# Layer 0's selective scan: VectorE weighs each scan's states one scan later, with five state buffers

## The chip, the cores and the metric

The kernel runs on one core of a Trainium2 chip. The metric is the device time of one execution in microseconds (us); the kernel before takes 15601.95 us, the median of three runs (15600.6 to 15609.41). Five engines work side by side, each through its own instructions in order: TensorE (PE, with its weight loads PEld), VectorE (DVE), ScalarE (ACT), GpSimd (POOL) and SyncE (SP), which issues DMAs. They wait for one another through semaphores.

## The reference

The program is four layers over an image of 2 x 64 x 64 positions with 128 channels; only layer 0 is touched. Its core is a selective scan along four orders of the 4096 positions of each image (kk = 0 to 3; orders 2 and 3 run backward, 1 and 3 by columns), with 256 channels and 16 states for each:

```
def step(h, inp):
    ut, dt, bt, ct = inp
    dA = jnp.exp(dt[..., None] * A4)
    h = dA * h + (dt * ut)[..., None] * bt[:, :, None, :]
    y = jnp.einsum('bkdn,bkn->bkd', h, ct)
    return (h, y)
```

The results of the four orders, each with u * D added, are summed into one Y.

## The kernel before, in words

For each of the two images `layer0` first computes U (channels on partitions, two halves of 128), then runs the scan stage (lines 247 to 420), then normalises Y and projects it. The stage walks 32 chunks of T = 512 positions, in the order kk = 0, 2, 1, 3 and eight chunks each (`todo`, line 330); a chunk walks its 16 states n. One state's tiles hold both halves, 128 x 2 x 512 numbers. One state is:

- POOL: S = du * (row n of B) (line 376), then for all but a direction's first chunk the state carried over from the chunk before is added into one column (lines 381, 382). `du` is dt * u; rows of B come by DMA, four at a time, in `br`.
- ACT: dA = exp(dt * A) in two halves (line 385), into one of two PSUM tiles `dAs`.
- DVE: the scan over both halves, in place in S (line 387).
- ACT: a copy of the last column of the state before into `stt`, for the next chunk (line 389).
- DVE: M = S * (row n of C) (line 401). The row, `pcn`, is a PSUM tile that TensorE fills by a product of `cs` with a selector (`c_row`, line 343). There is one such tile, so the next row waits for M to have read it.
- PE: the row of the next state, then four passes that add both halves of M into the PSUM tile `yp` through the identity (line 419).

At n = 0 `add_up` (line 346) first adds the finished `yp` of the chunk before into Y: for kk 0 by two ACT copies (line 354), for kk 2 by two DVE additions (line 356), for kk 1 and 3 by two strided ones (line 350). There is one `yp` tile, so only then can two products with `dd` (line 398) start the new one with u * D.

Beside the states runs the `prologue` of a later chunk (line 260), a generator; a step of it is issued after each state's M. It starts at n = 12 for the chunk two ahead: two steps copy U into `uc` (ACT), one makes the product `px`, one copies it to `xd` and `cs` and sends B's rows to DRAM, and in the next chunk's states follow softplus for dt (ACT with two table loads, and POOL at lines 299, 308, 311, 318, 320) and du (POOL, line 322).

The order on every engine is the order of the program text (`manual_schedule`, line 358). S has four buffers, M three.

Of the kernel before, what the change touches and what calls it, by code (L numbers as in the profile page):

```python
# [16 lines left out]
F32 = mybir.dt.float32  # L17
# [3 lines left out]
ALU = mybir.AluOpType  # L21
# [4 lines left out]
P = 128  # L26
# [132 lines left out]
def layer0(k):  # L159
    tc, nc, ins, X = k.tc, k.nc, k.ins, k.X  # L160
    T = N
    NC = L // T
    with ExitStack() as es:
# [34 lines left out]
        for b in range(B):  # L198
            Xb = X[:, b * NTB : (b + 1) * NTB, :]
            with ExitStack() as e2:  # L200
                pre = e2.enter_context(tc.tile_pool(name=f"l0p{b}", bufs=1))
                wk = e2.enter_context(tc.tile_pool(name=f"l0w{b}", bufs=3))
# [44 lines left out]
            with ExitStack() as e2:  # L247
                ch = e2.enter_context(tc.tile_pool(name=f"l0h{b}", bufs=2))
                sm = e2.enter_context(tc.tile_pool(name=f"l0s{b}", bufs=1))
                wk = e2.enter_context(tc.tile_pool(name=f"l0k{b}", bufs=3))  # L250
# [9 lines left out]
                def prologue(kk, c, got):  # L260


                    uc = ch.tile([P, 2, T], F32, name="uc")
                    for h in range(2):
                        if kk % 2:
                            src = U[:, h, :].rearrange("p (g i w j) -> p w g j i", g=4, i=16, w=4)[:, c // 2, 2 * (c % 2) : 2 * (c % 2) + 2]
                            for g in range(2):
                                nc.scalar.copy(uc[:, h, g * 256 : (g + 1) * 256].rearrange("p (j i) -> p j i", j=16), src[:, g])
                        else:
                            src = U[:, h, (c // 2) * 1024 : (c // 2 + 1) * 1024].rearrange("p (i w j) -> p w i j", i=16, w=4)  # L270
                            for g in range(2):
                                nc.scalar.copy(uc[:, h, g * 256 : (g + 1) * 256].rearrange("p (i j) -> p i j", i=16), src[:, 2 * (c % 2) + g])
                        yield
                    px = ps.tile([P, N], F32, name="pd", tag="ps")
                    for h in range(2):
                        nc.tensor.matmul(px, w_xp[:, h, kk, :], uc[:, h, :], start=h == 0, stop=h == 1)
                    yield
                    xd = ch.tile([P, T], F32, name="xd")
                    nc.scalar.copy(xd, px)
                    bc = bcp.tile([16, T], F32, name="bc")  # L280
                    nc.sync.dma_start(out=bc, in_=xd[112:128, :])

                    cs = ch.tile([80, T], BF16, name="cs")
                    nc.scalar.copy(cs, xd[:80])


                    dt = ch.tile([P, 2, T], F32, name="dt")
                    du = ch.tile([P, 2, T], F32, name="du")
                    e = sm.tile([P, 2, T], F32, name="e")
                    u = sm.tile([P, 2, T], F32, name="u")  # L290
                    for h in range(2):
                        bias = k.v("dt_b")[:, kk * 2 + h : kk * 2 + h + 1]
                        pd = ps.tile([P, N], F32, name="pd", tag="ps")
                        nc.tensor.matmul(pd, w_dt[96:104, kk, h * P : (h + 1) * P], xd[96:104, :], start=True, stop=True)
                        yield
                        if h == 1:
                            yield
                            r = sm.tile([80, T], F32, name="r")
                            nc.gpsimd.tensor_tensor(r, xd[:80], cs, ALU.subtract)
                        nc.scalar.activation(e[:, h, :], pd, AF.Abs, bias=bias)  # L300
                        nc.scalar.activation(dt[:, h, :], pd, AF.Relu, bias=bias)
                    yield
                    nc.scalar.copy(cs[32:64], r[32:64])
                    nc.scalar.copy(cs[64:80], r[64:80])
                    nc.scalar.activation(e, e, AF.Exp, scale=-1.0)
                    yield
                    yield
                    nc.gpsimd.tensor_tensor(r[64:80], r[64:80], cs[64:80], ALU.subtract)
                    nc.scalar.activation(u, e, AF.Identity, bias=1.0)
                    yield  # L310
                    nc.gpsimd.tensor_tensor(dt, dt, e, ALU.add)
                    nc.scalar.copy(cs[64:80], r[64:80])
                    nc.scalar.activation(e, u, AF.Ln)
                    yield
                    nc.scalar.activation(u, u, AF.Identity, bias=-1.0)
                    yield
                    yield
                    nc.gpsimd.tensor_tensor(e, e, u, ALU.subtract)
                    yield
                    nc.gpsimd.tensor_tensor(dt, dt, e, ALU.add)  # L320
                    yield
                    nc.gpsimd.tensor_tensor(du, dt, uc, ALU.mult)

                    ea = ch.tile([P, 16, 2], F32, name="ea")
                    f = T - 1 if kk >= 2 else 0
                    for h in range(2):
                        nc.scalar.activation(ea[:, :, h], an[:, kk * 2 + h, :], AF.Exp, scale=dt[:, h, f : f + 1])
                    got.append((uc, bc, cs, dt, du, ea))

                todo = [(kk, ci) for kk in (0, 2, 1, 3) for ci in range(NC)]  # L330
                at = lambda i: (todo[i][0], NC - 1 - todo[i][1] if todo[i][0] >= 2 else todo[i][1])
                ready = []
# [8 lines left out]
                def c_row(cs, n):  # L341
                    o = pc_.tile([P, T], F32, name="pcn")
                    nc.tensor.matmul(o, sel[:, n, :], cs, start=True, stop=True)  # L343
                    return o

                def add_up(kk, c, yp):
                    for h in range(2):
# [3 lines left out]
                        else:  # L351
# [3 lines left out]
                            else:  # L355
                                nc.vector.tensor_tensor(o, yp[:, h, :], o, ALU.add)

                with tc.manual_schedule():
                    rows, pcn, last, save = spread(ready[0][1], 0), c_row(ready[0][2], 0), None, None
                    soon = []  # L360
                    for it, (kk, ci) in enumerate(todo):
                        c = at(it)[1]
                        uc, bc, cs, dt, du, ea = ready.pop()
# [8 lines left out]
                        for n in range(16):  # L372
                            if n % 4 == 0:
                                br = rows
                            S = wk.tile([P, 2, T], F32, name="S", bufs=4)
                            nc.gpsimd.tensor_tensor(S, du, br[:, n % 4, :].unsqueeze(1).to_broadcast([P, 2, T]), ALU.mult)  # L376
                            if ci > 0:
                                if n in (0, 2):

                                    m = slice(0, 14) if n == 0 else slice(14, 16)  # L380
                                    nc.gpsimd.tensor_tensor(stt[:, m], stt[:, m], ea[:, m], ALU.mult)
                                nc.gpsimd.tensor_tensor(S[:, :, f], S[:, :, f], stt[:, n, :], ALU.add)
                            dA = dAs[n % 2]
# [6 lines left out]
                                save = None  # L390
                            if ci < NC - 1:
                                save = stt[:, n, :], (S[:, :, 0] if kk >= 2 else S[:, :, T - 1])
                            if n == 0:
                                if last is not None:
                                    add_up(*last)
                                yp = py.tile([P, 2, T], F32, name="yp")
                                for h in range(2):
                                    nc.tensor.matmul(yp[:, h, :], dd[:, kk * 2 + h, :], uc[:, h, :], start=True, stop=False)
                                last = kk, c, yp
                            M = wk.tile([P, 2, T], F32, name="M")  # L400
                            nc.vector.tensor_tensor(M, S, pcn.unsqueeze(1).to_broadcast([P, 2, T]), ALU.mult)  # L401
                            if n == 12 and it + 2 < len(todo):
                                soon.append(prologue(*at(it + 2), ready))
                            for steps in soon:
                                next(steps, None)
                            if n == 14 and it + 1 < len(todo):
                                for _ in soon.pop(0):
                                    pass
                            if n < 15:
                                pcn = c_row(cs, n + 1)  # L410
                            elif ready:
                                pcn = c_row(ready[0][2], 0)
                            if n % 4 == 2:
                                if n < 14:
                                    rows = spread(bc, n // 4 + 1)
                                elif ready:
                                    rows = spread(ready[0][1], 0)
                            for h in range(2):
                                nc.tensor.matmul(yp[:, h, :], k.ident, M[:, h, :], start=False, stop=n == 15)  # L419
                    add_up(*last)  # L420

            with ExitStack() as e2:
                wk = e2.enter_context(tc.tile_pool(name=f"l0f{b}", bufs=3))
# [35 lines left out]
                behind = None  # L459
                for q in range(8):  # L460
# [3 lines left out]
                    behind = got  # L464
# [252 lines left out]
def layer2(k, x1, x3, rs, sh, wdr, mdr):  # L717
# [21 lines left out]
    with ExitStack() as es:  # L739
# [390 lines left out]
        def make_inputs(r):  # L1130
            i, r = divmod(r, 256 // R)
            if i < len(todo):
                d = r * R
                gi, q = divmod(d, DG)
                if q == 0:
                    Ss[i, gi] = sp.tile([P, 2, DG, T], F32, name="S")
                S = Ss[i, gi][:, :, q : q + R, :]
# [427 lines left out]
```

## Time and profile before

| | |
|---|---|
| three runs, median | 15601.95 us |
| the profiled execution's own time | 15611.47 us |
| its span, first to last instruction | 15609.7 us |
| granted TensorE clock, mean of the span | 0.913 |
| scan stage, first image | 143.0 to 2070.3 us |
| scan stage, second image | 2263.6 to 4194.7 us |
| POOL in both stages | 3279.03 us busy of 3858.40 |
| ACT in both stages | 2370.75 us busy |
| PE in both stages | 2577.80 us busy |

A group's line of the profile names the source line, the engine, the operation, the tiles written and read (`out<-in`), their shapes, how often it ran, then its busy time and the mean of one in ns, then the idle time of the engine just before these instructions, and what ended most of it. A line of a timeline has the start and the duration in us, and in brackets the idle time of the engine before it and what ended that. An engine's instructions may overlap a little in such rows, since a duration includes the end of the pipe.

### The profile page before, as it was taken

Reading aid. Unit: us, or ns where it says so; the run is one execution under the profiler, and the core shown is the slowest. Engines: PE = TensorE matmul, PEld = TensorE weight load, DVE = VectorE, ACT = ScalarE, POOL = GpSimd, SP = SyncE. Lnnn points to the kernel's source line nnn. Section 1 sums busy time; section 2 is a strip of 40 time slices with the busy share of each in tenths; the row PEclk is TensorE's granted clock in tenths of the full one; section 3 lists DMA queues with packets and bytes.
Section 4 is the critical chain, followed back from the end, with each engine's and each line's share of the span. In section 5 each row is a group of like instructions: output and inputs, shape, how many; then the busy total and the mean of one; then the engine's idle time right before and its main releaser. Section 6 shows DMA issues by size and latency. Waiting matters only on the chain.

```text
span 15609.7 us, 191436 instructions
## 1 busy us (share of the span) xinstructions
PE 11894.2 (76%) x69838; PEld 7117.6 (46%) x69838; DVE 13768.3 (88%) x12194; ACT 9829.7 (63%) x15891; POOL 13474.0 (86%) x5144
## 2 busy tenths in 40 slices
PE   6666676666677645486976978979788899898897
PEld 2222232222367512154653645646445555555565
DVE  7999979999853499999999999999999999999964
ACT  5666646666410177777777777777777777777752
POOL 6888848888578699999999999999999999999960
PEclk9999999999988767697987989989999999999998
DMA  2111111211175445465655556656666666666643
GB/s 82 71 71 70 67 60 71 73 68 71 63 226 160 137 151 163 154 195 177 204 188 169 195 179 194 202 182 200 194 193 195 192 197 202 192 196 199 188 160 130
DMA packets 1211438, 2373.47 MB, mean 152 GB/s; under 512 B 346744, under 2 KB 923896, under 8 KB 1044352
## 3 DMA queue, kind: packets, MB, share of 16 engines
q1 hardware_dynamic: 1163072, 2206.74, 43.2%
q0 software_dynamic: 46560, 153.18, 3.3%
q8 instruction: 552, 9.04, 0.2%
q14 instruction: 390, 3.19, 0.1%
q10 hardware_dynamic: 864, 1.32, 0.0%
HBM read 2018.49 MB, written 342.41 MB: 151 GB/s over the span
## 4 chain that ended last, share of the span: by engine, by line
POOL 35%; PE 14%; DVE 11%; DMA 3%; ACT 2%; issue 2%; SPq 0%; POOLq 0%; ACTq 0%; DVEq 0%
POOL S L1139 34%; DVE S L1195 10%; PE pef L1023 7%; PE Z L1157 2%; PE acc L996 2%; DMA row<-drow 2%; PE pw L822 1%; POOL S L1145 1%; ACT dA L1193 1%; ACT ze L1163 1%; DMA w<-in_w_b_dram 0%; PE acc L1058 0%; DMA e<-mdr 0%; ACT e L1003 0%; DMA w<-in_w_c_dram 0%
## 5 line engine op out<-in xcount | busy, mean ns | idle before, releaser
L1195 DVE TENSOR_TENSOR_SCAN S<-dA,S 128x512 f32<-128x512 f32 x8192 | 9226.4, 1200 | 397.2 <-ACT dA L1193 208.2
L1139 POOL TENSOR_TENSOR S<-row,g 128x4096 f32<-128x4096 f32 x1024 | 9102.2, 8895 | 280.6 <-DMA row<-drow 232.4
L1193 ACT ACTIVATE dA<-row,a_t 128x512 f32<-128x512 f32 x8192 | 5616.2, 692 | 2158.3 <-DVE S L1195 2123.3
L1157 PE MATMUL Z<-S,cv 128*32 128x256 f32 x32768 | 2504.9, 436 | 1486.0 <-ACT ze L1163 1227.3
L1023 PE MATMUL pef<-hk,ur 128*128 128x256 f32 x14336 | 3507.0, 388 | 137.8 <-ACT e L1003 122.0
L1023 PEld LDWEIGHTS pef<-hk,ur 128*128 128x128 f32 x14336 | 2642.0, 191 | 1076.6 <-issue 562.1
L376 POOL TENSOR_TENSOR S<-du,br 128x1024 f32<-128x1024 f32 x1024 | 2409.7, 2356 | 282.7 <-DVE M L401 164.9
L387 DVE TENSOR_TENSOR_SCAN S<-dA,S 128x1024 f32<-128x1024 f32 x1024 | 2338.0, 2283 | 161.2 <-ACT dA L385 101.9
L1157 PEld LDWEIGHTS Z<-S,cv 128*32 128x32 f32 x32768 | 1002.0, 121 | 2695.7 <-issue 1286.1
L419 PE MATMUL yp<-M,ident 128*128 128x512 f32 x4096 | 1974.5, 604 | 2.9 <-DVE M L401 2.9
L419 PEld LDWEIGHTS yp<-M,ident 128*128 128x128 f32 x4096 | 789.9, 193 | 2147.7 <-issue 2112.7
L385 ACT ACTIVATE dA<-dt,an 128x511 f32<-128x511 f32 x2048 | 1406.5, 687 | 194.2 <-DVE S L387 148.1
L401 DVE TENSOR_TENSOR M<-S,pcn 128x1024 f32<-128x1024 f32 x1024 | 1250.4, 1221 | 151.9 <-PE pcn L343 51.9
L343 PE MATMUL pcn<-cs,sel 80*128 80x512 bf16 x1024 | 394.7, 385 | 1183.6 <-DVE M L401 1174.7
L1163 ACT COPY ze<-Z 128x512 f32<-128x512 f32 x1024 | 1123.0, 1097 | 236.9 <-PE Z L1157 204.6
L996 PE MATMUL acc<-e,mw 128*128 128x512 f32 x1920 | 1047.6, 634 | 31.2 <-ACT e L1003 30.5
L598 POOL DMA_INDIRECT G<-table,idx x576 | 810.8, 1408 | 202.6 <-issue 170.3
L1023 PEld LDWEIGHTS pef<-hd,ur 128*128 128x128 f32 x4096 | 758.2, 194 | 491.5 <-issue 236.0
L1023 PE MATMUL pef<-hd,ur 128*128 128x256 f32 (+1 forms) x4096 | 877.8, 341 | 101.6 <-ACT e L1003 95.3
L389 ACT COPY stt<-S 128x2 f32<-128x2 f32 x896 | 169.3, 189 | 1067.9 <-DVE S L387 1064.8
L605 DVE TENSOR_TENSOR G<-G,wt 128x4608 f32<-128x4608 f32 x64 | 317.6, 4963 | 579.6 <-DMA G<-table,idx 486.4
L613 ACT COPY vt<-pv 128x512 f32<-128x512 f32 (+1 forms) x192 | 88.4, 480 | 864.9 <-remote 598.0
(331 smaller groups left out, 8503.8 us busy)
## 6 DMA issues: line engine op xcount, KB each, us to landing
row<-drow SPq DMA_DIRECT2D x1024, 1024.0 KB
br<-bc SPq DMA_DIRECT2D x256, 1024.0 KB
zd<-ze SPq DMA_DIRECT2D x1024, 256.0 KB
hk<-in_phi_dram SPq DMA_DIRECT2D x128, 576.5 KB
hk<-in_phi_dram SPq DMA_DIRECT2D x96, 704.5 KB
hd<-in_phi_dram SPq DMA_DIRECT2D x512, 128.5 KB
mw<-wdr SPq DMA_DIRECT2D x480, 128.0 KB
hk<-in_phi_dram SPq DMA_DIRECT2D x160, 320.5 KB
```

The lines of the kernel that those rows point to most:

```text
L376: nc.gpsimd.tensor_tensor(S, du, br[:, n % 4, :].unsqueeze(1).to_broadcast([P, 2, T]), ALU.mult)
L385: nc.scalar.activation(dA[:, h, rest], dt[:, h, rest], AF.Exp, scale=an[:, kk * 2 + h, n : n + 1])
L387: nc.vector.tensor_tensor_scan(flat, dflat, flat, 0.0, ALU.mult, ALU.add)
L401: nc.vector.tensor_tensor(M, S, pcn.unsqueeze(1).to_broadcast([P, 2, T]), ALU.mult)
L419: nc.tensor.matmul(yp[:, h, :], k.ident, M[:, h, :], start=False, stop=n == 15)
L996: nc.tensor.matmul(acc.rearrange("p a s -> p (a s)"), ms[f][:, o, :], e, start=box["first"], stop="whole" in box and (f, o) == todo[-1])
L1023: nc.tensor.matmul(pe[:, a, 256 - n :], ur[:, par, j, :], h[:, at : at + n], start=i == 0, stop=i + 1 == len(mm))
L1139: nc.gpsimd.tensor_tensor(S, row.unsqueeze(1).to_broadcast([P, 2, R, T]), g.unsqueeze(2).to_broadcast([P, 2, R, T]), ALU.mult)
L1157: nc.tensor.matmul(Z[32 * j : 32 * j + 32, q], cv[:, h, s], S[:, h, :, s], start=h == 0, stop=h == 1)
L1163: nc.scalar.copy(ze.rearrange("p q t e -> p q e t"), Z)
L1193: nc.scalar.activation(dA, row[:, j % R, :], AF.Exp, scale=a_t[:, h, d : d + 1])
L1195: nc.vector.tensor_tensor_scan(s, dA, s, 0.0, ALU.mult, ALU.add)
```

## The change

A new helper `weigh` makes M from a given S, issues the next row of C, and sums M into `yp`. It is called for the state before (`behind`) after the scan of this one, across the chunks' bounds too, and once more behind the loop. What belonged to n = 0 (adding up, starting `yp`) goes to n = 1. S gets a fifth buffer. `prologue` starts at n = 11 instead of 12 and has one more empty step behind the first product, so that the copy to `xd` stays where it was; `xd` has one buffer instead of two.

```
                     for h in range(2):
                         nc.tensor.matmul(px, w_xp[:, h, kk, :], uc[:, h, :], start=h == 0, stop=h == 1)
                     yield
-                    xd = ch.tile([P, T], F32, name="xd")
+                    yield
+                    xd = ch.tile([P, T], F32, name="xd", bufs=1)
...
+                def weigh(S, yp, n, then=None):
+                    M = wk.tile([P, 2, T], F32, name="M")
+                    nc.vector.tensor_tensor(M, S, pcn.unsqueeze(1).to_broadcast([P, 2, T]), ALU.mult)
+                    row = c_row(*then) if then is not None else None
+                    for h in range(2):
+                        nc.tensor.matmul(yp[:, h, :], k.ident, M[:, h, :], start=False, stop=n == 15)
+                    return row
...
-                    soon = []
+                    soon, behind = [], None
...
-                            S = wk.tile([P, 2, T], F32, name="S", bufs=4)
+                            S = wk.tile([P, 2, T], F32, name="S", bufs=5)
...
-                            if n == 0:
+                            if n == 1:
                                 if last is not None:
                                     add_up(*last)
                                 yp = py.tile([P, 2, T], F32, name="yp")
...
-                            M = wk.tile([P, 2, T], F32, name="M")
-                            nc.vector.tensor_tensor(M, S, pcn.unsqueeze(1).to_broadcast([P, 2, T]), ALU.mult)
-                            if n == 12 and it + 2 < len(todo):
+                            if behind is not None:
+                                pcn = weigh(behind, yp, (n - 1) % 16, (cs, n))
+                            behind = S
+                            if n == 11 and it + 2 < len(todo):
                                 soon.append(prologue(*at(it + 2), ready))
                             for steps in soon:
                                 next(steps, None)
...
-                            if n < 15:
-                                pcn = c_row(cs, n + 1)
-                            elif ready:
-                                pcn = c_row(ready[0][2], 0)
...
-                            for h in range(2):
-                                nc.tensor.matmul(yp[:, h, :], k.ident, M[:, h, :], start=False, stop=n == 15)
+                    weigh(behind, yp, 15)
                     add_up(*last)
```

## The prediction

> **What bounds the kernel now.** I read the page first: engines, then the costliest groups. VectorE (DVE) has the largest share. Two of its groups belong to layer 0's scan: the scan itself (L387) and M = S times a row of C (L401).
>
> ```profile
> PE 11894.2 (76%) x69838; PEld 7117.6 (46%) x69838; DVE 13768.3 (88%) x12194; ACT 9829.7 (63%) x15891; POOL 13474.0 (86%) x5144
> ...
> L387 DVE TENSOR_TENSOR_SCAN S<-dA,S 128x1024 f32<-128x1024 f32 x1024 | 2338.0, 2283 | 161.2 <-ACT dA L385 101.9
> L401 DVE TENSOR_TENSOR M<-S,pcn 128x1024 f32<-128x1024 f32 x1024 | 1250.4, 1221 | 151.9 <-PE pcn L343 51.9
> ```
>
> Then the two scan stages alone, one window for each batch (143.0 to 2070.3 and 2263.6 to 4194.7 us); this line is their sum.
>
> ```profile
> sum 3858.40, PE 2577.80 PEld 1022.66 DVE 3596.95 ACT 2370.75 POOL 3279.03; mean PE 1288.90 PEld 511.33 DVE 1798.48 ACT 1185.37 POOL 1639.51
> ```
>
> DVE works 3597 of 3858 us, so its 261 idle us are what can be won here, beside the overlap told below. The groups say what they are: 102 on dA from ScalarE, 52 on a row of C, about 8 on other ScalarE ends, and the rest, some 99, has no releaser. VectorE's timeline shows that rest (start, duration):
>
> ```profile
> 804.58 1.22 DVE L401 TENSOR_TENSOR M<-S,pcn 128x1024 f32<-128x1024 f32 x1
> 805.72 2.28 DVE L387 TENSOR_TENSOR_SCAN S<-dA,S 128x1024 f32<-128x1024 f32 x1
> 808.11 1.22 DVE L401 TENSOR_TENSOR M<-S,pcn 128x1024 f32<-128x1024 f32 x1
> 809.25 2.28 DVE L387 TENSOR_TENSOR_SCAN S<-dA,S 128x1024 f32<-128x1024 f32 x1
> ```
>
> A scan starts 0.08 us before the M ahead of it is over (804.58 + 1.22 = 805.80 against 805.72): neighbours overlap. But M starts 0.105 us after the scan ended, because it reads that scan's S and waits for its end. A state takes 2.283 + 0.105 + 1.221 - 0.084 = 3.525 us. Layer 2 shows two scans in a row without such a wait:
>
> ```profile
> 5598.99 21.26 DVE L1195 TENSOR_TENSOR_SCAN S<-dA,S 128x512 f32<-128x512 f32 x19
> ```
>
> 19 scans of 1.20 us in 21.26: start to start (21.26 - 1.20) / 18 = 1.114, an overlap of 0.085.
>
> **The change, part by part.** I write n for the state and take every duration from the rows above or from timelines.
>
> 1. *M one scan later.* VectorE's order becomes scan n, M of n-1, scan n+1. M no longer waits for its neighbour's end, only for its row of C, so both joints should overlap by 0.084: a state takes 2.283 + 1.221 - 0.168 = 3.336 us, 0.189 less. Of 1024 M, 46 stand behind an add-up, not a scan, and 34 behind the late row of C: 944 x 0.189 = **178 us won**. The nearest other joint, a scan followed by an add-up that waits for TensorE, lies between -0.08 and -0.013 us (1828.00 + 2.28 against 1830.27 is the second); by that end it is 944 x 0.118 = 111. I take 178, since the new M's wait is long over, as in layer 2.
>
> The Trainium skill speaks against this: "VectorE: DVE Perf Modes", section "The DRAIN you can't avoid", holds that an instruction pays for the emptying of the pipe with or without a semaphore behind it, and gives eight copies that took as long with one semaphore as with eight. By it this part would be worth nothing and the sum some 47 us; the trace's two kinds of joint (-0.084 and +0.105 us) say otherwise here.
>
> 2. *The row of C and the sums one state later (n = 1).* In the chunks of kk 1 and 3 VectorE adds up Y, TensorE starts yp with two dd products, and the next row of C queues behind them and a product of the prologue:
>
> ```profile
> 1830.27 2.43 DVE L350 TENSOR_TENSOR Y<-yp,Y 128x512 f32<-128x512 f32 x2
> ...
> 1832.85 3.49 PE L398 MATMUL yp<-uc,dd 128*128 128x512 f32 x4 [2.61 <-DVE Y L350]
> ...
> 1836.27 1.12 PE L294 MATMUL pd<-xd,w_dt 8*128 8x512 f32 x2
> ...
> 1837.32 0.39 PE L343 MATMUL pcn<-cs,sel 80*128 80x512 bf16 x1
> ...
> 1837.74 1.22 DVE L401 TENSOR_TENSOR M<-S,pcn 128x1024 f32<-128x1024 f32 x1 [1.73 <-PE pcn L343]
> ```
>
> After, the prologue's product of state 0 stands ahead of dd and runs while VectorE adds, so only dd is before the row. With T the end of scan 1: add-up T to T+2.35, dd from T+2.58; M of 0 to T+3.55 (its row is long there); scan 2 to T+5.75; M of 1 due at T+5.67. TensorE is then idle 1.5 us ahead of dd, not 2.6. All 30 dd groups behind 1.16 to 1.38 us of idling take 1.98 us, most behind 2.6 take 3.5 (half pace). Row ready at T+2.58+1.98+0.4 = T+4.96: no wait; with slow dd at T+6.5, a wait of 0.85. I take none: 51.9 us plus the overlap regained, 34 x 0.084, is **55 won**; the other end is 55 - 30 x 0.93 = 27.
>
> 3. *ScalarE at n = 7* (54 times 1.19 us in the row L387). ScalarE's copy waits for the end of scan 5, and two table loads stand before the dA of state 7:
>
> ```profile
> 1851.77 0.19 ACT L389 COPY stt<-S 128x2 f32<-128x2 f32 x1 [1.07 <-DVE S L387]
> ...
> 1854.97 1.28 ACT L385 ACT_TABLE_LOAD   x1
> 1856.26 1.42 ACT L385 ACTIVATE dA<-dt,an 128x511 f32<-128x511 f32 x2
> ```
>
> From scan 5's end (1851.74) to scan 7's start (1857.78) are 6.04 us, unchanged after. VectorE fills 4.77 of them now (1.27 lost, overlap included) and 2 x 0.189 less after (1.65 lost): 54 x 0.38 = **20 given back**. The stall that is next late, dA of state 4, has 0.90 us in hand, 0.52 after.
>
> 4. *ScalarE in kk 0*, where add-ups are its copies and now stand ahead of dA of state 2, no longer ahead of dA of state 1 with two activations between:
>
> ```profile
> 323.12 1.07 ACT L354 COPY Y<-yp 128x512 f32<-128x512 f32 x2 [2.67 <-PE yp L419]
> ```
>
> With E the end of the last M of the chunk before (320.94 here): copies E+2.18 to 3.26, dA E+3.14 to 4.58, scan 2 at E+4.68. VectorE could start it at E+3.25 (scan 1, M of 0), so 1.43 us are lost, against 2.38 now (2.30 in the row): 14 x 0.95 = **13 won**.
>
> 5. *Ends.* In each batch the last two M stand side by side and the second's row waits for the first: 0.14 + 0.38 + 0.08, twice, **1 us given back**.
>
> 6. *Hidden by VectorE, costed at nothing.* Five buffers: S of n+4 now waits for M of n as S of n+4 did, M of n-1 being the last read: with M one later and one buffer more, GpSimd (POOL) may run exactly as far ahead as before. Its tight place is state 12: it waits for ScalarE's u (L318 at 1858.82, 1.04 us after scan 7 starts), then does three 2.35 us steps of the prologue and S of 10, 11, 12, and is done 15.77 us after scan 7's start. Scan 12 starts 17.63 us after it now (1.86 in hand) and 5 x 3.336 = 16.68 after: 0.91 in hand. Per chunk POOL has 52 us of work and 1.5 of small gaps, under the 56.3 I expect. The copies into uc one state earlier: dA of state 12 is done 3.35 us after scan 10's end (0.2 + 0.5 of ea + 1.17 + 1.44) and is due after 4.39. The xd copy stays at n = 15, and the first product, one state earlier, spares it the wait of 1.47 us; dA of state 0 had 0.52 in hand, so nothing is won. The DMAs of SP (bc, the rows of B) are issued at the same n behind the same work. If a cover fails, each 0.1 us late per chunk costs 6 us.
>
> Sum: 178 + 55 + 13 - 20 - 1 = **225 us**. From the profiled execution's own 15611.5 us (span 15609.7) that gives 15386; that execution lies 9.5 us above the median, so 15602 - 225 = **15377**. Cross-check: the idle left is 54 x 1.57 + 14 x 1.35 + 6 x 1.53 for the starts of directions, 113; busy 3597 - 944 x 0.084 = 3518; 3631 against 3858, 227 less.
>
> **Rivals.**
> - *The joint does not close* (it is the chip's, or the wait on the row, not on the scan). Then 225 - 178 = 47 won: 15555. For it: every M here has the gap. Against it: M behind add-ups overlaps like all else (1832.60 against 1831.46 + 1.24), and those read nothing fresh. 4%.
> - *POOL becomes the bound* at S of 12: its 0.91 us are gone if its pin comes 1 us later. A shortfall of 1 us in 56 chunks: 225 - 56 = 169 won, 15433. Against it: it waits 66.7 us on u in 31 chunks, so there it has time left. 9%.
> - *Slower: TensorE falls to half pace.* A state's row and four passes of sums then take 3.84 us (3837.41 to 3841.25), above 3.34 and 3.525: VectorE waits 0.50 us a state. With 225 to lose that decides from 450 of 1024 states, and all of them would end at 225 - 512 = 287 us slower, 15889. For it: 2.6 us of idling slowed dd. Against: the granted clock is 0.97 in the stage with 1.43 us of idling a state, and that shrinks. 4%.
> - *No change:* what VectorE wins it waits again for ScalarE or POOL. POOL's 52 us and ScalarE's 38 a chunk speak against it. 3%.
>
> **How the numbers follow.** The forecast has 80%. Its range: at least 158 us won (part 1 by its other joint), 15444; at most 225 + 20 (ScalarE's wait does not grow) + 10 (the spread of the runs shown), 15347. POOL as the bound lies inside. Faster by over 0.2% (31 us, about what can be told from no change here): 80 + 9 + 4 = 93%; within it 3%; slower 4%.
>
> **What would show it.** Right: M starts some 0.08 us before the scan ahead of it ends; a state takes 3.34 us; "PE pcn" is gone from M's idle time; L387's idle before n = 7 is near 1.57 us; the two stages' windows sum to about 3632 us and DVE is busy 97% of them. Wrong: a gap of 0.1 us that stays, scans that wait for POOL's S at n = 11 to 13, dd still at 3.5 us, or a granted clock under 0.9 in the stage.

## The result: slower by 0.36%

The changed kernel takes 15661.11 us (median of eight runs, 15648.09 to 15664.23), the kernel before 15604.47 beside it (eight runs, 15593.37 to 15609.41). The ratio is 1.0036, with a 95% interval of 1.0027 to 1.0044: slower. The forecast was 15377, with a range of 15347 to 15444: wrong in size and in sign.

### The profile after

The profiled execution's span is 15661.0 us (before 15609.7), its mean granted TensorE clock 0.895 (before 0.913). The page of the changed kernel, the engines and the two groups of the scan:

```profile
PE 12083.7 (77%) x69838; PEld 7190.8 (46%) x69838; DVE 13675.8 (87%) x12194; ACT 9838.0 (63%) x15891; POOL 13474.3 (86%) x5144
...
L397 DVE TENSOR_TENSOR_SCAN S<-dA,S 128x1024 f32<-128x1024 f32 x1024 | 2340.8, 2286 | 346.8 <-ACT dA L395 236.7
...
L362 DVE TENSOR_TENSOR M<-S,pcn 128x1024 f32<-128x1024 f32 x1024 | 1228.5, 1200 | 50.7 <-PE pcn L344 50.7
```

M does what was foreseen: of its 151.9 idle us the 99 without a releaser are gone, and DVE's busy time falls by 92.5. But the scan's idle time has grown from 161 to 347, most of it on dA. Now the scan stage alone, from the first scan to the end of the last M of each image: first the two stages and their sum in the changed kernel, then the sum before (1.2 us more than the one shown above, whose first window ended where the last M began). The columns are the stretch, its length, PE, PEld, DVE, ACT and POOL busy with counts, granted clock, DMA share and GB/s.

```profile
142.70:2101.20 1958.50, 1397.39 (x2927) 549.50 (x2926) 1753.44 (x1076) 1187.31 (x2133) 1638.00 (x1201) 0.90 0.18 68
2291.70:4249.40 1957.70, 1395.82 (x2927) 548.98 (x2926) 1753.29 (x1076) 1187.28 (x2133) 1638.08 (x1201) 0.90 0.18 68
sum 3916.20, PE 2793.21 PEld 1098.48 DVE 3506.73 ACT 2374.59 POOL 3276.07; mean PE 1396.60 PEld 549.24 DVE 1753.37 ACT 1187.29 POOL 1638.04
```

```profile
143.00:2071.50 1928.50, 1283.49 (x2927) 509.38 (x2926) 1798.99 (x1076) 1185.40 (x2133) 1639.51 (x1201) 0.97 0.19 70
...
sum 3859.60, PE 2577.80 PEld 1022.66 DVE 3598.14 ACT 2370.75 POOL 3279.03; mean PE 1288.90 PEld 511.33 DVE 1799.07 ACT 1185.37 POOL 1639.51
```

The stages are 56.6 us longer, which is the whole loss (the span grew by 51.3). VectorE works 91 us less in them and idles 148 more: 3916.2 - 3506.7 = 409.5 against 261.5. PE does the same instructions in 215 us more, at a clock of 0.90 instead of 0.97. VectorE's idle time by place, in us over both stages:

| ahead of | before | after |
|---|---|---|
| M, behind its own scan | 99 | 0 |
| scan 0 of a chunk (the stages' first left out) | 9 | 153 |
| scan 1 (before) or 2 (after), in kk 0 and the chunk behind it | 33 | 45 |
| scan 7 | 64 | 86 |
| M whose row of C stands behind dd | 52 | 51 |
| the add-up, on `yp` | 0 | 63 |
| the rest | 4 | 11 |

So the 99 was won, and more was lost in two new places: scan 0, and the add-up. The waits of ScalarE name the first one. Its rows in the changed kernel, then before (engine, line waited at, line waited for; us in total, times, longest):

```profile
ACT e L301 <- PE pd L295: 179.6, 108, 4.9
ACT cs L285 <- PE pcn L344: 160.2, 60, 3.3
ACT xd L280 <- PE pd L276: 107.7, 63, 3.6
```

```profile
ACT xd L279 <- PE pd L276: 108.0, 63, 3.8
...
ACT e L300 <- PE pd L294: 62.4, 73, 5.5
```

The middle row is new: in 60 chunks ScalarE's cast into `cs` waits for a row of C. The timeline shows one chunk's end, in the changed kernel (the columns are start and duration):

```profile
1730.68 2.29 DVE L397 TENSOR_TENSOR_SCAN S<-dA,S 128x1024 f32<-128x1024 f32 x1
...
1731.35 0.58 ACT L280 COPY xd<-pd 128x512 f32<-128x512 f32 x1 [1.47 <-PE pd L276]
...
1732.88 1.20 DVE L362 TENSOR_TENSOR M<-S,pcn 128x1024 f32<-128x1024 f32 x1
...
1734.13 0.38 PE L344 MATMUL pcn<-cs,sel 80*128 80x512 bf16 x1 [0.88 <-DVE M L362]
...
1734.59 0.62 ACT L285 CAST cs<-xd 80x512 bf16<-80x512 f32 x1 [2.66 <-PE pcn L344]
...
1735.12 1.41 ACT L395 ACTIVATE dA<-dt,an 128x511 f32<-128x511 f32 x2
...
1736.15 1.12 PE L295 MATMUL pd<-xd,w_dt 8*128 8x512 f32 x2
...
1736.62 2.29 DVE L397 TENSOR_TENSOR_SCAN S<-dA,S 128x1024 f32<-128x1024 f32 x1 [2.55 <-ACT stt L399]
...
1740.08 0.38 PE L344 MATMUL pcn<-cs,sel 80*128 80x512 bf16 x1 [2.81 <-DVE M L362]
...
1740.30 2.88 PE L365 MATMUL yp<-M,ident 128*128 128x512 f32 x4
...
1743.22 2.41 DVE L351 TENSOR_TENSOR Y<-yp,Y 128x512 f32<-128x512 f32 x2 [0.95 <-PE yp L365]
```

The scan at 1730.68 is that of state 15. M of 14 follows it at 1732.88 and ends at 1734.08, and only then may TensorE fetch row 15, for there is one `pcn`. That row is the last reader of this chunk's `cs`. There are two `cs`, and the cast is for the chunk two ahead, into the same one; so it waits for the row (1734.59, 2.66 us behind the copy to `xd`). Behind the cast stands dA of state 0, and scan 0 starts 2.55 us late. (The bracket names the small copy that stands behind dA on ScalarE; dA ended 0.09 us ahead of the scan: 1735.12 + 1.41 against 1736.62.) In the same place before, row 15 was issued in state 14, and the cast followed `xd` at once; its dA ended 0.52 us ahead of scan 0:

```profile
1824.94 0.58 ACT L279 COPY xd<-pd 128x512 f32<-128x512 f32 x1 [1.48 <-PE pd L276]
1825.56 0.62 ACT L284 CAST cs<-xd 80x512 bf16<-80x512 f32 x1
1826.08 1.40 ACT L385 ACTIVATE dA<-dt,an 128x511 f32<-128x511 f32 x2
...
1828.00 2.28 DVE L387 TENSOR_TENSOR_SCAN S<-dA,S 128x1024 f32<-128x1024 f32 x1
```

The last three lines of the changed kernel show the second place. While VectorE stands still, TensorE gets no M and idles 2.81 us; then its four passes into `yp` take 2.88 us (1.88 before), and VectorE waits 0.95 for the sum, with `dd` and the next row behind it.

### The profile page after: what moved, and what is told of

Read it like the earlier page. It is cut to its first block, busy times and chain, and to the rows that moved or that the text cites. A ratio compares the mean times of both kernels' runs of the same rounds, so it can differ in the third digit from the quotient of the medians.

```text
span 15661.0 us, 190284 instructions
## 1 busy us (share of the span) xinstructions
PE 12083.7 (77%) x69838; PEld 7190.8 (46%) x69838; DVE 13675.8 (87%) x12194; ACT 9838.0 (63%) x15891; POOL 13474.3 (86%) x5144
## 4 chain that ended last, share of the span: by engine, by line
POOL 34%; PE 13%; DVE 12%; DMA 3%; issue 2%; ACT 2%; SPq 1%; POOLq 0%; DVEq 0%; ACTq 0%
POOL S L1146 33%; DVE S L1202 11%; PE pef L1030 7%; PE Z L1164 2%; PE acc L1003 2%; DMA row<-drow 1%; PE pw L829 1%; POOL S L1152 1%; ACT dA L1200 1%; ACT ze L1170 0%; DMA w<-in_w_b_dram 0%; SPq L853 0%; PE acc L1065 0%; DMA e<-mdr 0%; ACT e L1010 0%
## 5 line engine op out<-in xcount | busy, mean ns | idle before, releaser
L365 PE MATMUL yp<-M,ident 128*128 128x512 f32 x4096 | 2114.6, 641 | 0.0
L365 PEld LDWEIGHTS yp<-M,ident 128*128 128x128 f32 x4096 | 838.6, 205 | 2166.3 <-issue 2129.7
```

## The experiments

**Theory A**: the cast's wait on row 15 costs the stall at scan 0, and through TensorE's pace most of the rest. **Theory B**: there is a second wait. TensorE's products for dt (L295) are issued in the prologue's step, behind M of 14, row 15 and the sums; ScalarE's activations for softplus wait for them, ahead of dA of state 1. **Theory C**: the joint between VectorE's instructions closed for another reason than the fresh S, or something else in the new order (five buffers) costs. (The recorded expectations letter their own theories, anew in each run.) The kernels x1 to x4 shared one chip, x5 to x8 another, x9 and x10 the first again.

### x1: a third buffer for cs

```
-                    cs = ch.tile([80, T], BF16, name="cs")
+                    cs = ch.tile([80, T], BF16, name="cs", bufs=3)
```

> The changed kernel with a third buffer for cs and nothing else. Its trace has ScalarE's cast into cs waiting 2.66 us (60 times) for the row of C of state 15, which is now issued a state later and still reads the old cs; dA of state 0 is late by 2.55 us behind it. Theory A, two waits one behind the other: the cast's wait goes, but TensorE's first product for dt (pd) still stands behind the row of state 15 and the sums of M of 14, so the two activations that read pd hold up dA of state 1 until about the same moment; the lost 2.5 us move from n = 0 to n = 1 and the time stays within 30 us of the changed kernel's 15661. Theory B, the cs buffer alone: 60 x 2.55 = 153 us are won, 15510, and down to 15390 if TensorE's half pace after the stall goes too (68 us of waits ahead of the add-ups, 50 us ahead of the row of state 1).

Measured: 15529.25 us (15520.63 to 15532.61) against 15598.99, ratio 0.9954 (0.9937 to 0.9971). The row `cs <- pcn` is gone, and scan 0 no longer waits. The chunk shown above, in this kernel:

```profile
1736.80 2.29 DVE L397 TENSOR_TENSOR_SCAN S<-dA,S 128x1024 f32<-128x1024 f32 x1
...
1738.95 1.12 PE L295 MATMUL pd<-xd,w_dt 8*128 8x512 f32 x2
...
1740.11 0.69 ACT L301 ACTIVATE e<-pd,pv 128x512 f32<-128x512 f32 x1 [3.30 <-PE pd L295]
...
1741.27 1.41 ACT L395 ACTIVATE dA<-dt,an 128x511 f32<-128x511 f32 x2
...
1742.78 2.29 DVE L397 TENSOR_TENSOR_SCAN S<-dA,S 128x1024 f32<-128x1024 f32 x1 [2.58 <-ACT stt L399]
```

The stall has moved by one state: now scan 1 waits 2.58 us, because ScalarE waits 3.30 for the product (theory B). VectorE loses 144 us there; in the changed kernel it lost 153 at scan 0. The 132 us won against that kernel stand in waits for what TensorE makes: the add-ups' falls from 63 us to 0.5, scan 2's of kk 0 from 45 to 1, M's on its row from 51 to 37, and the clock in the stage rises from 0.90 to 0.94. So neither recorded theory held whole: the first had the stall's move right but expected the time to stay near 15661, the second expected 15510 but no move.

### x2: x1, and the prologue's steps ahead of M

```
+                            if n == 11 and it + 2 < len(todo):
+                                soon.append(prologue(*at(it + 2), ready))
+                            for steps in soon:
+                                next(steps, None)
                             if n == 1:
...
                                 pcn = weigh(behind, yp, (n - 1) % 16, (cs, n))
                             behind = S
-                            if n == 11 and it + 2 < len(todo):
-                                soon.append(prologue(*at(it + 2), ready))
-                            for steps in soon:
-                                next(steps, None)
```

> The changed kernel with a third buffer for cs and with the prologue's step of each state issued ahead of M, its row and its sums, so that TensorE takes the prologue's products before it waits for M of the state before. Theory A: both waits go, the joints stay closed, and what the prediction worked out should come: about 200 us under the kernel before (225 less some 25, since the product that kept TensorE busy during the strided add-up is ahead of the sums again and dd runs at half pace for kk 1 and 3), so some 15400. Theory B: the order of steps matters little; the same time as with the third buffer alone. Theory C, TensorE's pace is the cause by itself and not the waits: the granted clock in the stage stays near 0.90 and the time near 15660.

Measured: 15372.77 us (15371.15 to 15386.3), ratio 0.9858 (0.9841 to 0.9874). Both waits are gone, and so is the loss. The sum of the stages (bounds as above), and the scan's group on the page:

```profile
sum 3638.80, PE 2585.82 PEld 1033.43 DVE 3496.61 ACT 2368.11 POOL 3274.16; mean PE 1292.91 PEld 516.72 DVE 1748.31 ACT 1184.06 POOL 1637.08
```

```profile
L397 DVE TENSOR_TENSOR_SCAN S<-dA,S 128x1024 f32<-128x1024 f32 x1024 | 2338.6, 2284 | 175.1 <-ACT dA L395 117.5
```

VectorE idles 3638.8 - 3496.6 = 142 us, where the changed kernel idles 410. PE is back at 2586, near the 2578 before.

### x3: the kernel before, with row 15 fetched late

```
+                            if n == 15:
+                                c_row(cs, 15)
                             for steps in soon:
                                 next(steps, None)
```

> The kernel before, with the row of C of state 15 made a second time in state 15, behind M of 15 and ahead of the prologue's step, its result unused. The cast into cs then waits for a row that comes after the scan of 15 and an M, as in the changed kernel, with the old order of scan and M. Theory (the late release of cs alone makes dA of state 0 late): 0.55 + 0.62 + 1.40 + 0.1 = 2.6 us lost ahead of the first scan of some 60 chunks, 140 to 170 us slower than the kernel before, 15745 to 15775, with TensorE's clock lower after the stall. Rival (the stall comes from the new order and not from cs): within 20 us of 15602.

Measured: 15768.1 us (15766.56 to 15773.72), ratio 1.0109 (1.0092 to 1.0125): 169 us slower. The kernel before gets the wait with nothing else of the change:

```profile
ACT cs L284 <- PE pcn L343: 185.3, 60, 3.4
```

Scan 0 waits 2.55 us in it, as in the changed kernel. Theory A's mechanism is shown by itself, and so is its price where the joint is the old one: of 165 us more idling in the stages, 144 are at scan 0. M's wait on its row also grows, from 52 to 76 us; the additional row (60 times 0.38 us on TensorE) may have a part in that.

### x4: the kernel before, M made from du

```
-                            nc.vector.tensor_tensor(M, S, pcn.unsqueeze(1).to_broadcast([P, 2, T]), ALU.mult)
+                            nc.vector.tensor_tensor(M, du, pcn.unsqueeze(1).to_broadcast([P, 2, T]), ALU.mult)
```

> The kernel before with M = du * row of C in place of S * row of C, so that M reads nothing that the scan ahead of it wrote: the sums leave the scan out. Order, counts and shapes are those of the kernel before. Theory (the 0.105 us ahead of M is the wait for the scan's end): both joints overlap by 0.08, 0.189 us a state, 178 us less the 20 that ScalarE's wait at n = 7 takes back, so about 15445. Rival (the joint belongs to the row of C in PSUM or to the two instructions): still 0.1 us ahead of M, 15602.

Measured: 15418.88 us (15414.73 to 15424.47), ratio 0.9886 (0.9869 to 0.9902): 180 us won. M stands directly behind its scan in this kernel too, but reads a tile that was finished long ago:

```profile
1739.10 2.28 DVE L387 TENSOR_TENSOR_SCAN S<-dA,S 128x1024 f32<-128x1024 f32 x1
1741.30 1.20 DVE L401 TENSOR_TENSOR M<-du,pcn 128x1024 f32<-128x1024 f32 x1
1742.41 2.28 DVE L387 TENSOR_TENSOR_SCAN S<-dA,S 128x1024 f32<-128x1024 f32 x1
```

1739.10 + 2.28 = 1741.38 against 1741.30: M now starts 0.08 us before the scan's end, and a state takes 3.31 us (1742.41 - 1739.10) instead of 3.53. The gap was the wait for the neighbour's end and nothing else: neither the order nor five buffers. M itself takes 1198 ns, 23 less than before. That is some 24 us over 1024 states, which my expectation lacked.

### x5: x1, and only step 15 of the prologue ahead of M

```
+                            for steps in soon if n == 15 else ():
+                                next(steps, None)
                             if n == 1:
...
-                            for steps in soon:
+                            for steps in soon if n != 15 else ():
```

> The changed kernel with a third buffer for cs, and of the prologue's steps only that of n = 15 (xd, the cast into cs, TensorE's first product for dt) issued ahead of M, its row and its sums; all others stay behind. In the run with the third buffer alone the stall had gone to n = 1: two activations wait 3.3 us for that product, which stands behind the sums of M of 14, and dA of state 1 is late by 2.58 us in 56 chunks. Theory A (that one product's place is the rest of the loss): 56 x 2.58 = 145 us and some 20 to 35 us of waits for the row of state 1 go, 15350 to 15385. Rival (the place of several steps counts, the first product's too): half of that or less, 15450 to 15530.

Measured: 15391.53 us (15385.1 to 15398.03) against 15603.17, ratio 0.9864 (0.9847 to 0.988), 7 us above the range expected. One step's place in TensorE's order is worth 15529 - 15392 = 137 us: theory B is shown with its place. By its ratio this kernel is not told apart from x2, whose other steps stand ahead too.

### x6: x2, but step 0 behind M

```
-                            for steps in soon:
+                            for steps in soon if n != 0 else ():
                                 next(steps, None)
...
+                            for steps in soon if n == 0 else ():
+                                next(steps, None)
```

> As the run with all steps first and three buffers for cs (15373), but the step of n = 0 stays behind, so that its product keeps TensorE busy while VectorE adds up Y, as the prediction had it. Theory: dd comes after 1.5 us of idling and not 2.6, runs at full pace, and the 13 us of waits for the row of state 1 go: 15355 to 15370. Rival (the pace of dd does not go by that idle time): 15373 again, with the same waits at n = 1.

Measured: 15381.46 us (15374.6 to 15390.52), ratio 0.9857 (0.9841 to 0.9874): not told apart from x2. This puts the second product just ahead of `dd`, as part 2 of the prediction had it, and shortens the idling ahead of `dd` in kk 1 and 3 from 2.6 to some 1.6 us. The pace did not follow. A product of the prologue, then `dd`:

```profile
1738.67 1.12 PE L295 MATMUL pd<-xd,w_dt 8*128 8x512 f32 x2
1741.38 3.56 PE L412 MATMUL yp<-uc,dd 128*128 128x512 f32 x4 [1.59 <-DVE Y L351]
```

Of 28 such groups behind 1.54 to 1.60 us of idling only 5 took under 2.2 us; the median is 3.49. M still waits for its row, 21.5 us in all against 15.8 in x2, so the kernel gains nothing by it.

### x7: x2 with four buffers for S

```
-                            S = wk.tile([P, 2, T], F32, name="S", bufs=5)
+                            S = wk.tile([P, 2, T], F32, name="S", bufs=4)
```

> As the run with all steps first and three buffers for cs (15373), with four buffers for S. Theory of the prediction's part 6 (five buffers give GpSimd the lead that four gave before): S of n now waits for M of n-4, which comes behind scan n-3, so GpSimd's lead shrinks by one state. S of 9 is then ready 2.6 us after scan 7 starts, the step on u behind it starts 1.6 us later than its present 1.04, S of 12 is ready 17.3 us after scan 7 starts and due after 16.7: 0.6 us in some 56 chunks, 30 to 45 us slower, some 15410, with scans waiting for S at n = 11 to 13. Rival (GpSimd has time enough with four): 15373 within 15 us.

Measured: 15404.8 us (15398.04 to 15417.58), ratio 0.9875 (0.9858 to 0.9891): 32 us above x2 by the medians, a size that was expected. Only 9 of them show as scans that wait for POOL's S (at state 12, in eight chunks, 1.5 us in six of them; in x2 none there), and 9 as M on its row of C (24.6 us against 15.8). So POOL loses its margin there, as was thought. The two stages are 25 us longer, so some 7 of the 32 lie outside them, where the kernels do not differ; the rest is spread over small waits that I could not put down to POOL.

### x8: the kernel before with five buffers for S and one for xd

```
-                    xd = ch.tile([P, T], F32, name="xd")
+                    xd = ch.tile([P, T], F32, name="xd", bufs=1)
...
-                            S = wk.tile([P, 2, T], F32, name="S", bufs=4)
+                            S = wk.tile([P, 2, T], F32, name="S", bufs=5)
```

> The kernel before with five buffers for S and one for xd, and nothing else of the change. Both theories that put the loss into the order of M, row and prologue expect no difference, 15602 within 15 us: no scan waits for S in the kernel before. Rival (the single xd buffer makes ScalarE or the DMA of B's rows wait): 20 us or more slower.

Measured: 15602.53 us (ten runs, 15596.35 to 15612.54), ratio 0.9999 (0.999 to 1.0009). The buffers alone change nothing; with x4 theory C has fallen.

### x9: the product's wait removed, the cast's kept

Two `cs`, as in the change. At n = 15 the copy to `xd` and the first product for dt stand ahead of M of 14, row 15 and the sums; the cast into `cs` is a step of its own behind them.

```
                     xd = ch.tile([P, T], F32, name="xd", bufs=1)
                     nc.scalar.copy(xd, px)
...
-                    cs = ch.tile([80, T], BF16, name="cs")
-                    nc.scalar.copy(cs, xd[:80])
...
                         nc.tensor.matmul(pd, w_dt[96:104, kk, h * P : (h + 1) * P], xd[96:104, :], start=True, stop=True)
                         yield
+                        if h == 0:
+                            cs = ch.tile([80, T], BF16, name="cs")
+                            nc.scalar.copy(cs, xd[:80])
+                            yield
...
+                            for steps in soon if n == 15 else ():
+                                next(steps, None)
                             if n == 1:
```

> The changed kernel with two buffers for cs as it is. At n = 15 the copy to xd and TensorE's first product for dt are issued ahead of M, its row and its sums; the cast into cs stays behind them, after the row of state 15. So of the two waits only the cast's is left. Theory A (either wait alone costs about 2.6 us a chunk, and they overlap in the changed kernel): dA of state 0 is late by 2.55 us in 60 chunks as in the changed kernel, nothing waits at n = 1 beyond the usual, 60 x 2.63 = 158 us above the run with neither wait (15373), 15500 to 15560. Rival (once the product is first, the cast's wait is hidden): 15375 to 15400.

Measured: 15669.58 us (15655.3 to 15677.97) against 15598.71, ratio 1.0046 (1.003 to 1.0061). Neither expectation held: the cast's wait alone costs all that the change lost. The chunk's end in this kernel:

```profile
1739.17 1.12 PE L292 MATMUL pd<-xd,w_dt 8*128 8x512 f32 x2
...
1740.71 0.62 ACT L296 CAST cs<-xd 80x512 bf16<-80x512 f32 x1 [2.78 <-PE pcn L345]
...
1742.74 2.29 DVE L398 TENSOR_TENSOR_SCAN S<-dA,S 128x1024 f32<-128x1024 f32 x1 [2.67 <-ACT dA L396]
...
1746.19 0.38 PE L345 MATMUL pcn<-cs,sel 80*128 80x512 bf16 x1 [3.86 <-DVE M L363]
...
1746.41 3.12 PE L366 MATMUL yp<-M,ident 128*128 128x512 f32 x4
...
1749.57 2.42 DVE L352 TENSOR_TENSOR Y<-yp,Y 128x512 f32<-128x512 f32 x2 [1.22 <-PE yp L366]
```

The product runs early, the cast waits 2.78 us, scan 0 2.67. Then TensorE, with the product behind it, has nothing at all for 3.86 us, its passes slow down (3.12 us for four), and the add-up waits 1.22. I had expected the stall at scan 0 without these after-effects: the add-ups' wait is 63 us, as in the changed kernel, and M's on its row 54.6 us. With x1, x5 and the changed kernel this is a table of two waits:

| us | the product waits | it does not |
|---|---|---|
| the cast waits | 15661 (the change) | 15670 (x9) |
| it does not | 15529 (x1) | 15392 (x5) |

They do not add up. Either stalls VectorE once a chunk by about 2.6 us, both together no longer than one; the cast's comes first and also slows TensorE ahead of the add-up.

### x10: x2, and a later cast of the rest

In the prologue the last copy into `cs` moves from the step with Ln, ahead of dA of state 7, to an empty step two states on.

```
                     nc.gpsimd.tensor_tensor(dt, dt, e, ALU.add)
-                    nc.scalar.copy(cs[64:80], r[64:80])
                     nc.scalar.activation(e, u, AF.Ln)
                     yield
                     nc.scalar.activation(u, u, AF.Identity, bias=-1.0)
                     yield
+                    nc.scalar.copy(cs[64:80], r[64:80])
                     yield
```

> As the run with all steps first and three buffers for cs (15373), with ScalarE's cast of the last part of cs (0.61 us) moved from the step ahead of the two table loads to the empty step two states later. Theory of the prediction's part 3 (the 1.60 us that VectorE loses ahead of scan 7 are ScalarE's chain from the end of scan 5: copy, cast, table, Ln, table, dA): the chain is 0.61 us shorter, 54 x 0.61 = 33 us won, 15335 to 15350, and the wait at n = 7 reads 0.99 us. Rival (something else is ready as late, POOL's S or the row): 15373, wait still 1.6 us.

Measured: 15340.08 us (five runs, 15335.75 to 15344.49), ratio 0.9833 (0.9819 to 0.9846), as expected. Scan 7's wait falls from 1.60 to 0.97 us in this kernel:

```profile
1741.99 2.29 DVE L397 TENSOR_TENSOR_SCAN S<-dA,S 128x1024 f32<-128x1024 f32 x1 [0.97 <-ACT dA L395]
```

It is the fastest of all, 1.7% below the kernel before. Its list of waits seems to make POOL's S the next limit: 79.9 us in 32 places, 25 us more than in x2 (54.9 in six). That is a misnaming: 26 of the 32 are at scan 7, where dA ended 0.10 us ahead of the scan in all 54 chunks, while that state's S had been done for 3.4 us or more. Scan 7 still waits for ScalarE.

## Why the prediction was wrong

**Part 1, M one scan later: right.** Both joints are -0.084 us at the median in the changed kernel, and x4 shows that the wait for the neighbour's end made the gap. The rule of the Trainium skill as the prediction weighed it ("VectorE: DVE Perf Modes", section "The DRAIN you can't avoid": eight copies cost the same with one semaphore as with eight) would have had x4 gain nothing; it gained 180 us. The same section also says that an instruction that is not held starts earlier, which the prediction left out and x4's -0.08 us agrees with. Not foreseen was that M itself becomes 21 to 24 ns shorter.

**Part 6, "Hidden by VectorE, costed at nothing": this step failed.** It said "The xd copy stays at n = 15, and the first product, one state earlier, spares it the wait of 1.47 us; dA of state 0 had 0.52 in hand, so nothing is won." Three things are wrong in it. I counted states in the program's text, but TensorE's queue is tied to M, and M of n-1 now runs in state n. So the product with `w_xp`, issued a state earlier, ran as late as before, and `xd` still waits 1.47 us (107.7 us against 108.0). I did not ask who reads the old `cs` last: row 15, which moved a state later with M, while the cast into its buffer kept its place; dA of state 0 stood behind that cast with 0.52 us to spare against a wait of 2.66 (x3 and x9). And the products for dt at n = 15, which the kernel before issued between M and the row, were now behind the late row and the sums (x1 and x5). I had looked at S for the release of buffers, where the change itself added one, and not at the buffers that it left alone.

From x5 to x9 the cast's wait costs 15670 - 15392 = 278 us: some 150 at scan 0 itself (160 against 10), 61 at the add-ups (63 against 2), 33 at M's row (54.6 against 21.3), 19 at scan 2 of kk 0 (38 against 19), the rest smaller.

**Part 2, the row of C at n = 1: wrong.** M's wait stays at 51 us (52 before). In the changed kernel `dd` takes 3.75 us even behind 0.57 to 0.60 us of idling (each of 14 groups), all of it at half clock: TensorE had idled 2.81 us shortly before. Without that stall, in x6, `dd` behind 1.6 us of idling still took 3.49 at the median, where I had put 1.98. I had read the pace off the length of the gap just before; the last section shows what it went by. The wait falls to 16 us in x2 and 21.5 in x6 all the same; the 27 to 55 us that this part was to win are won there in part, and not for the reason given.

**Part 3, ScalarE at n = 7: right.** The wait grew to 1.60 us (86 us in all, in the changed kernel as in x2), 1.57 forecast, and x10 shows by 33 us that it is on the path.

**Part 4, ScalarE in kk 0: right only without the stall.** 1.36 us in x2, 1.35 forecast; in the changed kernel it is 45 us in all against 33 before, because `yp` comes late.

**Part 5** was right: the last M waits 0.47 us in each image. **POOL** and the five buffers in part 6 were right as well: in x2, beside the stages' starts, scans wait for S in two places, 1 us in all, and with four buffers 9 us more (x7).

Without the two waits the sum holds: x2 has stages of 3638.8 us against 3631 forecast, and a time of 15373 against 15377. Two errors lie in that agreement: M's 24 us, which I had not counted, and idle time of 142 us instead of 113.

**The rivals.** TensorE at half pace was among them, for all states and out of its own idling; what happened is that the cast's stall brought it about around the chunk's bounds. My fourth rival, a wait that eats what VectorE wins, came nearest, and was dismissed by busy sums (ScalarE's 38 us a chunk), which say nothing about one late cast. **Still open** are some 14 of the 32 us of x7, and when TensorE's clock comes back after a stall.

## What to carry to other kernels

Where one engine's work is moved later, everything that it releases moves with it: list for every tile that it or its followers read last who writes the next one, and whether that writer has moved too, above all for tiles that the change does not touch. Work that another engine queues behind the moved work moves along, so its place is to be read from that engine's timeline and not from the loop index. And between two instructions of one engine, the one that reads what its direct neighbour wrote pays for it: 0.19 us here, a thousand times over.

## What the runs showed of the hardware

- A VectorE instruction that reads the result of the one directly before it started 0.105 us after that one's end; one that does not, 0.083 us before it (x4, the same two instructions in the same order). Over the 944 joints of part 1 that makes 178 us. The reader was also some 23 ns longer in the record (1221 against 1198).
- Four of TensorE's passes went from 1.88 us to 2.88 and 3.12 behind idling of 2.81 and 3.86 us, and the granted clock of the stage from 0.97 to 0.90. The length of the idling just before does not decide it alone. The four `dd` products took under 2.2 us in 30 of 32 cases behind 1.16 to 1.38 us (x2), in 5 of 28 behind 1.54 to 1.60 (x6), in 3 of 32 behind more than 2.5 in the kernel before, but in 19 of 32 behind as much in x4.
- What it goes by is in the clock records of these traces. In the scan stages of the kernel before, the changed one and x6, each of 242 stretches at half pace lasts a whole multiple of 3.41 us, and all changes lie on one grid of such windows. The chunk's end shown above, window by window (bounds, length, PE busy with its count, granted clock, DMA share, GB/s):

```profile
1734.20:1737.62 3.42, 3.07 (x7) 1.00 0.52 216
1737.62:1741.03 3.41, 0.95 (x3) 1.00 0.00 0
1741.03:1744.44 3.41, 3.41 (x5) 0.50 0.82 308
1744.44:1747.86 3.42, 2.83 (x4) 0.50 0.02 5
1747.86:1751.27 3.41, 3.41 (x5) 0.50 0.00 0
1751.27:1754.68 3.41, 3.16 (x9) 1.00 0.00 0
```

The window in which TensorE stood still had 0.95 us of work, and the next three run at half pace. In the three kernels' stages all 178 full-pace windows with PE busy for under 40% were followed by one at half pace, of 870 with 70% or more none was, and of 1914 in between 64. So it matters how a gap falls on the windows: in x6 the five fast `dd` lie wholly in windows at full pace, and each of the 23 slow ones has at least 42% of its time in windows at half pace. The Trainium skill ("TensorE: Matmul & The Clock Gate", section "What's actually happening") holds that the clock goes by free-running windows of about 3.4 us; these traces agree, with 3.41 us, and show that a window need not be empty to cost the pace of the next.
